# PSUM in two rings: side products share the four score banks, the scan's transposes keep the other three

## The chip, the cores and the metric

One core of a Trainium2 chip runs one fused kernel. The metric is the device time in microseconds of that core. PE is TensorE (its weight loads are listed apart as PEld), DVE is VectorE, ACT is ScalarE, POOL is GpSimd and SP is the engine that issues most DMAs. Each engine has one queue and works it off in order.

## The reference

The input x is 4 images of 64 x 64 positions and 256 channels, in float32. Two layers follow each other.

```python
# layer 0: a gated block with a scan over 2x2 windows and a depthwise convolution
x_norm = layernorm(x); x_proj, z = split(x_norm @ in_proj_W)          # 256 -> 384 + 384
y_ssm = 0.5 * (scan_fwd(windows(x_proj)) + scan_bwd(windows(x_proj))) # 4 steps, 8 states per channel
y_conv = gelu(depthwise3x3(x_proj) @ pw_W)
y = (alpha * y_ssm + (1 - alpha) * y_conv) * silu(z) @ out_W
x = x + y
x = x + gelu(layernorm(x) @ fuse_W1 + b1) @ fuse_W2 + b2
# layer 1: attention over all 4096 positions of an image
f, g, h = x @ Wf + bf, x @ Wg + bg, x @ Wh + bh                       # 32, 32, 256 channels
out = gamma * (softmax(g @ f.T) @ h @ Wo + bo) + x
```

The scan's step is `state = exp(dt * a) * state + dt * b * x`, and its output is `sum(state * c)` over the 8 states.

## The kernel before, in words

Layer 0 works on 32 blocks of 512 positions (8 rows of an image), 8 blocks to an image. The work of a block is a Python generator that yields a cost in microseconds after each piece, and generators are interleaved by these costs, so that the program's order is a planned mixture; a scheduler of the building layer then fixes the order on each engine and adds the semaphores.

The scan of a block (`scan`, L394) is the backbone. For each of 24 steps and two directions, ACT computes decays (`decays`, L368), PE transposes them in three 128 x 128 pieces into a PSUM tile `pa` (`turned`, L434), DVE multiplies `pa` into the state (`decayed`, L442 and L446) and then updates output and state (L452, L461). Beside the scan, `side` (L688) runs the rest of the neighbouring blocks: layer norm and projections (`to_channels` L273, `head` L302, `gate` L317), the scan's inputs (`prepare` L334 to L354), the depthwise convolution on PE and DVE (L550, L567), `tail` with its matmuls (L598, L623, L643, L654, L667, L678). `inputs` (L389) and `merge` (L539) are transposes at the ends of a scan.

As soon as the first image is through layer 0, attention begins, and `attend` (L994) becomes the outer loop: for each block of 128 queries, 8 times four matmuls of exponentials with values into `acc` (L1008), then a piece of `weights` for the next queries, then 7.2 us worth of layer 0 (`fill(RATE)`). `weights` (L804) makes the next queries' exponentials in 8 such pieces: twice 16 small score matmuls (L816, 32 rows each, four side by side, each of the four into a bank of its own), the maximum over the keys by DVE (L824) and a copy to SBUF by ACT (L827); then the maximum over partitions by a transpose, a reduction and a broadcast (L836 to L844), and then four times an addition by DVE and an exponential by ACT (L847, L848). The exponential tiles `eq` have seven buffers. When layer 0 is through, `attend_late` (L972) and `late_weights` (L893) do the rest with 256 queries at a time.

PSUM has eight banks, which are handed out so:

- pool `ps`, a ring of three banks (`bank`, L144): every product of the side work, `inputs`, `merge`, and the scan's `pa` in all blocks but the first eight;
- pool `pss`, two pairs of two banks (`pair`, L156): the scores, and the two small tiles of the maximum. In the first eight blocks, before there are any scores, the scan's `pa` lie here, the two directions of a step in one pair (`place`, L420);
- pool `pso`, one bank: `acc`.

A tile's bank is free once the engine that reads it (DVE or ACT) is through, and PE, which works in order, waits at the first matmul into a bank that isn't free.

Of the kernel before, what the change touches and what calls it, by code (L numbers as in the profile page):

```python
# [23 lines left out]
ALU = mybir.AluOpType  # L24
# [35 lines left out]
def block_then_attention_kernel(  # L60
# [94 lines left out]

    def pair(i):  # L156
        return pss.tile([P, 2, TOK], F32, tag=f"pair{i}", name=f"pair{i}")

# [109 lines left out]
    def to_channels(dst, src):  # L268

        for k in range(KD):  # L270
            pt = bank()
            for t in range(4):
                nc.tensor.transpose(pt[:, t * P : (t + 1) * P], src[:, t, k * P : (k + 1) * P], ident)  # L273
            nc.scalar.copy(dst[:, k, :], pt)
            yield 0.44
# [15 lines left out]
    def head(at):  # L291

        xt = heads.pop(at)
        layernorm(xt, xt)
        yield 5.0
        xnT = two.tile([P, KD, TOK], F32, tag="xnT", name="xnT")
        yield from to_channels(xnT, xt)
        xc = three.tile([P, KI, TOK], F32, tag="xc", name="xc")
        for f in range(KI):
            pp = bank()  # L300
            for k in range(KD):
                nc.tensor.matmul(  # L302
                    pp, lhsT=win[:, k, f * P : (f + 1) * P], rhs=xnT[:, k, :],
                    start=(k == 0), stop=(k == KD - 1),
                )
            nc.scalar.activation(xc[:, f, :], pp, AF.Identity, bias=b_in[:, f : f + 1])
            yield 1.72
        heads[at] = xnT, xc
        ready["head"] = at

    def gate(at, whole):
        xnT = heads[at][0]
        zs = one.tile([P, KI, TOK], F32, tag="zs", name="zs")
        for f in range(KI):
            pz = bank()
            for k in range(KD):
                nc.tensor.matmul(  # L317
                    pz, lhsT=win[:, k, INNER + f * P : INNER + (f + 1) * P], rhs=xnT[:, k, :],
                    start=(k == 0), stop=(k == KD - 1),
                )  # L320
            nc.scalar.activation(zs[:, f, :], pz, AF.Silu, bias=b_in[:, KI + f : KI + f + 1])
            if not whole:
                yield 1.72
        gates[at] = zs
        if whole:
            yield 5.2

    def prepare(at):

        _, xc = heads[at]  # L330

        pj = bank()
        for k in range(KI):
# [3 lines left out]
        yield 2.58  # L337
        pbc = ps.tile([P, 4, 2, 64], F32, tag="ps", name="pbc")
        for t in range(4):
# [10 lines left out]
        for d in range(2):  # L350
            dts.append(two.tile([P, KI, TOK], F32, tag="dt", name="dt"))
            for f in range(KI):
                pd = bank()
                nc.tensor.matmul(  # L354
                    pd, lhsT=wdt[64 * d : 64 * d + RANK, f * P : (f + 1) * P],
                    rhs=proj[64 * d : 64 * d + RANK, :], start=True, stop=True,
                )
                nc.scalar.activation(dts[d][:, f, :], pd, AF.Silu, bias=v("dt_b_b" if d else "dt_b_f", f))
            if at >= NBLK:
                yield 1.7  # L360
# [33 lines left out]
    def scan(at, ensue):  # L394
# [22 lines left out]

        pairs = {}

        def place(d, j):  # L420

            if at >= NBLK:
                return bank()
            if j + d not in pairs:
                pairs[j + d] = pair((j + d) % 2)
            return pairs[j + d][:, d, :]

# [115 lines left out]
    def depthwise(ydw, dense):  # L543

        for f in range(KI):
            if f < dense:
                pc = bank()
                for tap in range(9):
                    dy, dx = divmod(tap, 3)
                    nc.tensor.matmul(  # L550
                        pc, lhsT=diags[9 * f + tap], rhs=xp[:, f, dy : dy + ROWS, dx : dx + W],
                        start=(tap == 0), stop=(tap == 8),
                    )
                    if tap in (2, 5):
                        yield 2.6
                nc.scalar.copy(ydw[:, f, :], pc)
                yield 2.6
                continue
# [28 lines left out]
    def tail(at):  # L587
# [7 lines left out]
        for f in range(KI):  # L595
            pw = bank()
            for k in range(KI):
# [20 lines left out]
        for t2 in range(2):  # L618
            po = ps.tile([P, 2, DIM], F32, tag="ps", name="po")
            for t1 in range(2):  # L620
                t = 2 * t2 + t1
                for k in range(KI):
                    nc.tensor.matmul(  # L623
                        po[:, t1, :], lhsT=yz[:, k, t * P : (t + 1) * P], rhs=wout[:, k, :],
                        start=(k == 0), stop=(k == KI - 1),
                    )
            nc.vector.tensor_tensor(xo[:, 2 * t2 : 2 * t2 + 2, :], po, xo[:, 2 * t2 : 2 * t2 + 2, :], ALU.add)
            yield 3.2
# [11 lines left out]
        for f in range(KF):  # L640
            pf = bank()
            for k in range(KD):
# [6 lines left out]
        for t2 in range(2):  # L649
            pq = ps.tile([P, 2, DIM], F32, tag="ps", name="pq")  # L650
            for t1 in range(2):
# [12 lines left out]
        yield from to_channels(xT, xo)  # L664
        pf = bank()
        for k in range(KD):
# [8 lines left out]
        for t in range(4):  # L675
            po = bank()
            for k in range(KD):
# [126 lines left out]
    def weights(b, q, es):  # L804
# [3 lines left out]
        for g in range(2):  # L808
            pr = [pair(i) for i in range(2)]

            with tc.high_priority():
                last = None
                for s in range(4):
                    at = g * TOK + s * P
                    for r in (2, 3, 0, 1):
                        ins = nc.tensor.matmul(  # L816
                            pr[r // 2][:, r % 2, s * P : (s + 1) * P], lhsT=fQ[CK * r : CK * (r + 1), at : at + P],
                            rhs=gq[CK * r : CK * (r + 1), :], start=True, stop=True,
                        )
                        last = behind(ins, last)  # L820
            mx = two.tile([P, 2, P], F32, tag="mx", name="mx")
            for a in range(2):
                e = ep.tile([P, 2, TOK], F32, tag="eq", name="eq")
                nc.vector.tensor_reduce(  # L824
                    mx[:, a, :], pr[a].rearrange("p r (s q) -> p q (r s)", s=4), AX.X, ALU.max
                )
                nc.scalar.copy(e, pr[a])  # L827
                es.append(e)
            if g == 0:
                mx0 = mx  # L830
            yield
            yield
        nc.vector.tensor_tensor(mx0, mx0, mx, ALU.max)
        pm = pair(0)
        for c in range(2):
            nc.tensor.transpose(pm[:, 0, c * P : (c + 1) * P], mx0[:, c, :], ident)  # L836
        nm = st.tile([P, 1], F32, tag="nm", name="nm")
        nc.vector.tensor_reduce(nm, pm[:, 0, :QB], AX.X, ALU.max, negate=True)
        nmb = two.tile([P, P], F32, tag="nb", name="nmb")
        nc.vector.tensor_copy(nmb, nm.to_broadcast([P, P]))  # L840
        pn = pair(1)
        nc.tensor.matmul(pn[:, 0, :P], lhsT=nmb, rhs=ident, start=True, stop=True)
        nb = two.tile([P, P], F32, tag="nb", name="nb")
        nc.scalar.copy(nb, pn[:, 0, :P])  # L844
        for n, e in enumerate(es):
# [47 lines left out]
    def late_weights(b, q, odd, es):  # L893
# [6 lines left out]
        for g in range(4):  # L900
            pr = [pair(i) for i in range(2)]
            for s in range(2):
                at = (g // 2) * TOK + (2 * (g % 2) + s) * P
                for r in range(4):
                    nc.tensor.matmul(  # L905
                        pr[r // 2][:, r % 2, s * QB : (s + 1) * QB], lhsT=fQ[CK * r : CK * (r + 1), at : at + P],
                        rhs=gq[CK * r : CK * (r + 1), :], start=True, stop=True,
                    )
            for a in range(2):
                pool, tag = SLOTS[8 * odd + 2 * g + a]  # L910
                e = pool.tile([P, 2, 2, QB], F32, tag=tag, name="eT")
                for j in range(2):
                    nc.scalar.copy(e[:, j], pr[a][:, j, :].rearrange("p (s q) -> p s q", s=2))  # L913
                if g == 0 and a == 0:
# [9 lines left out]
        nc.vector.tensor_tensor(m2, mx[:, 0, :], mx[:, 1, :], ALU.max)  # L924
        pm = pair(0)
        for c in range(2):
            nc.tensor.transpose(pm[:, 0, c * P : (c + 1) * P], m2[:, c * P : (c + 1) * P], ident)
        nm = st.tile([P, 2], F32, tag="nm", name="nm")
        nc.vector.tensor_reduce(
            nm, pm[:, 0, :QB].rearrange("p (c k) -> p c k", c=2), AX.X, ALU.max, negate=True  # L930
        )
# [3 lines left out]
        yield  # L935
        pn = pair(1)
        for c in range(2):
            nc.tensor.matmul(
                pn[:, 0, c * P : (c + 1) * P], lhsT=wide[:, c, :], rhs=ident, start=True, stop=True
            )  # L940
        nb = two.tile([P, QB], F32, tag="mx", name="nb")
        nc.scalar.copy(nb, pn[:, 0, :QB])  # L942
        for n, e in enumerate(es):
# [214 lines left out]
```

## Time and profile before

| | |
|---|---|
| time, median of 3 runs | 5544.09 us (5538.5 to 5545.41) |
| the profiled execution | 5536.67 us, of it 5534.9 us span |
| PE busy | 5111.2 us (92%) |
| DVE busy | 4585.6 us (83%) |
| ACT busy | 3626.7 us (66%) |

The profile shows one execution. It is read in three stages: up to about 1000 us layer 0 runs alone (the first image), from there to about 4566 us layer 0 of the other images runs beside attention, and from 4566 us on attention runs alone. A row of the groups of instructions gives the line, the engine, what it writes and reads, the count, the busy time, the mean duration of one, and the idle time of its engine just before with what ended it. PE runs a float32 matmul as two instructions of the trace, a transpose as one. A row of the waits names who waited for whom, the sum in microseconds, how often, and the longest.

### The profile page before, as it was taken

How to read it: one execution, taken by the hardware profiler on the slowest of the kernel's cores; microseconds unless marked ns; L12 is line 12 of the kernel's file. 1: busy time of each engine (PE TensorE's matmuls, PEld its weight loads, DVE VectorE, ACT ScalarE, POOL GpSimd, SP SyncE). 2: the span in 40 equal slices, each digit the busy share in tenths (PEclk: the TensorE clock that was granted, in tenths of full speed). 3: DMA queues.
4: the chain of work that ended last, by engine and by line, in shares of the span. 5: the costliest groups of instructions: out<-in, count | busy, mean ns of one | idle time of the engine just before them, and what ended most of it. 6: DMA issues, size and time to landing. Idle time of an engine off the chain costs nothing. (4 is left out here: it accounts for less than half of the span.)

```text
span 5534.9 us, 77215 instructions
## 1 busy us (share of the span) xinstructions
PE 5111.2 (92%) x27476; PEld 3619.7 (65%) x27476; DVE 4585.6 (83%) x8158; ACT 3626.7 (66%) x5248; POOL 202.6 (4%) x304
## 2 busy tenths in 40 slices
PE   7888888899999999999999999999999999999999
PEld 4555555566666666666666666666666667888887
DVE  6888888889888898988988888899988885666665
ACT  5666667666666777777667776777677654555444
POOL 0000000000000000000000000000000000000000
PEclk7999999899999999999999999999999999999999
DMA  1000100133333333433333333333333335555554
GB/s 46 25 22 24 32 18 18 50 109 112 102 111 114 108 107 115 118 110 114 113 109 108 117 113 115 109 106 117 115 115 106 105 106 160 148 144 146 147 146 138
DMA packets 333121, 558.42 MB, mean 101 GB/s; under 512 B 51904, under 2 KB 86976, under 8 KB 332736
## 3 DMA queue, kind: packets, MB, share of 16 engines
q1 hardware_dynamic: 330160, 551.52, 33.7%
q8 instruction: 218, 3.57, 0.3%
q10 hardware_dynamic: 2576, 1.97, 0.1%
q14 instruction: 167, 1.37, 0.1%
HBM read 494.49 MB, written 58.79 MB: 100 GB/s over the span
## 5 line engine op out<-in xcount | busy, mean ns | idle before, releaser
L1008 PE MATMUL acc<-vt,eq 128*128 128x257 f32 x4864 | 1231.9, 388 | 24.8 <-issue 14.0
L373 ACT ACTIVATE e<-dt,a_sc 128x384 f32<-128x384 f32 x1536 | 855.1, 608 | 356.5 <-PE bank L434 270.8
L1008 PEld LDWEIGHTS acc<-vt,eq 128*128 128x128 f32 x4864 | 893.9, 194 | 234.5 <-issue 115.4
L452 DVE SCALAR_TENSOR_TENSOR y<-p,bc,y 128x384 f32<-128x384 f32 x1536 | 941.2, 613 | 1.2
L986 PE MATMUL bank<-vt,eT 128*128 128x257 f32 x2496 | 624.7, 382 | 0.0
L461 DVE SCALAR_TENSOR_TENSOR h<-u,bc,p 128x384 f32<-128x384 f32 x1024 | 620.5, 623 | 0.2
L434 PEld LDWEIGHTS bank<-ident,e 128*128 128x128 f32 x3456 | 412.1, 142 | 256.7 <-DVE p L442 74.0
L434 PE MATMUL bank<-ident,e 128*128 128x128 f32 x3456 | 511.6, 278 | 70.8 <-DVE p L442 46.6
L986 PEld LDWEIGHTS bank<-vt,eT 128*128 128x128 f32 x2496 | 467.0, 189 | 80.7 <-issue 12.9
L446 DVE TENSOR_TENSOR p<-bank,h 128x384 f32<-128x384 f32 x768 | 408.7, 548 | 104.0 <-PE bank L434 101.4
L827 ACT COPY eq<-pair 128x1024 f32<-128x1024 f32 x304 | 302.9, 1010 | 221.8 <-DVE mx L824 108.3
L373 ACT ACT_TABLE_LOAD x310 | 397.7, 1283 | 7.8 <-PE bank L434 2.6
L848 ACT ACTIVATE eq<-eq 128x1024 f32<-128x1024 f32 x304 | 317.5, 1055 | 116.3 <-DVE eq L847 108.6
L824 DVE TENSOR_REDUCE mx<-pair 128x128 f32<-128x1024 f32 x304 | 362.0, 1213 | 24.1 <-PE pair L816 24.0
L847 DVE TENSOR_TENSOR eq<-eq,nb 128x1024 f32<-128x1024 f32 x304 | 361.8, 1227 | 18.7 <-ACT nb L844 17.8
L918 DVE TENSOR_TENSOR mx<-mx,eT 128x512 f32<-128x512 f32 x364 | 251.9, 692 | 140.4 <-ACT eT L913 110.6
L913 ACT COPY eT<-pair 128x512 f32<-128x512 f32 x416 | 213.1, 598 | 184.3 <-PE pair L905 184.3
L567 DVE SCALAR_TENSOR_TENSOR ydw<-xp,vec,ydw 128x512 f32<-128x512 f32 x448 | 320.8, 744 | 2.9
L598 PE MATMUL bank<-ydw,wpw 128*128 128x512 f32 x576 | 274.4, 608 | 21.6 <-DVE p L446 17.5
L442 DVE SCALAR_TENSOR_TENSOR p<-bank,bc,u 128x384 f32<-128x384 f32 x384 | 233.7, 608 | 67.2 <-PE bank L434 67.0
L945 DVE TENSOR_TENSOR eT<-eT,nb 128x1024 f32<-128x1024 f32 x208 | 238.5, 1218 | 46.9 <-ACT nb L942 46.9
L550 PE MATMUL bank<-xp,dw 128*128 128x512 f32 x576 | 274.6, 603 | 1.7 <-DVE xc L540 1.7
(150 smaller groups left out, 7775.5 us busy)
## 6 DMA issues: line engine op xcount, KB each, us to landing
vt<-vod SPq DMA_DIRECT2D x1632, 257.0 KB, 2.8
vod<-vst SPq DMA_DIRECT2D x32, 514.0 KB, 4.3
xo<-in_x_dram SPq DMA_DIRECT2D x256, 64.0 KB, 2.6
xt<-in_x_dram SPq DMA_DIRECT2D x256, 64.0 KB, 1.9
x1d<-xo SPq DMA_DIRECT2D x32, 512.0 KB, 2.9
res<-x1d SPq DMA_DIRECT2D x76, 128.0 KB, 2.7
out_dram<-res SPq DMA_DIRECT2D x304, 32.0 KB, 1.6
fgd<-fg SPq DMA_DIRECT2D x32, 256.0 KB, 2.1
```

What stands on the lines that cost most here:

```text
L373: nc.scalar.activation(e[:, f, :], dts[d][:, f, lo : lo + 3 * P], AF.Exp, scale=a_sc[:, d, f * NST + n : f * NST + n + 1],)
L434: nc.tensor.transpose(pa[:, f * P : (f + 1) * P], es[d, n][:, f, off : off + P], ident)
L446: nc.vector.tensor_tensor(p, pa[:, :INNER], hs[d], ALU.mult)
L452: nc.vector.scalar_tensor_tensor(y[:, t, :], p, bc[:, t, d, NST + n : NST + n + 1], y[:, t, :], ALU.mult, ALU.add)
L461: nc.vector.scalar_tensor_tensor(hs[d], u[d][:, t, :], bc[:, t, d, n : n + 1], p, ALU.mult, ALU.add)
L567: nc.vector.scalar_tensor_tensor(o, x_tap, w_tap, o, ALU.mult, ALU.add)
L824: nc.vector.tensor_reduce(mx[:, a, :], pr[a].rearrange("p r (s q) -> p q (r s)", s=4), AX.X, ALU.max)
L827: nc.scalar.copy(e, pr[a])
L847: nc.vector.tensor_tensor(e8, e8, nb.unsqueeze(1).broadcast_to([P, 8, P]), ALU.add)
L848: nc.scalar.activation(e, e, AF.Exp)
L986: nc.tensor.matmul(sums[c][:, : DIM + 1], lhsT=e[:, r % 2, s, c * P : (c + 1) * P], rhs=vt[:, s, :], start=(n == 0 and s == 0), stop=(n == ...
L1008: nc.tensor.matmul(acc[:, : DIM + 1], lhsT=es[k // 2][:, k % 2, a : a + P], rhs=vt[:, s, :], start=(n == 0 and s == 0), stop=(n == 2 * NI ...
```

## The change

The two pairs become four single banks with the tags q0 to q3. `aside()` hands them out in turn. All side products (L273, L302, L317, L334, L340, L354, L550, L598, L623, L643, L654, L667, L678) and the two small tiles of the maximum now take the next of these four. The ring of three is left to the scan's `pa`, `inputs` and `merge`; in the first eight blocks every fourth `pa` goes to the bank of `acc`, which is not yet in use. The scores take all four banks at once (`four`), the bank that was handed out last coming first, and do not move the turn.

In `weights`, ACT copies each score bank by itself (four copies of 512 columns instead of two of 1024), and DVE takes the maximum a piece later, from the copies in SBUF instead of from PSUM. The number of pieces stays 8; the steps L833 to L844 come one piece earlier. `late_weights` takes the four single banks too; its copies were of single banks already.

```diff
-    def pair(i):
-        return pss.tile([P, 2, TOK], F32, tag=f"pair{i}", name=f"pair{i}")
+    turn = [0]
+    def aside(shape=(P, TOK)):
+        i = turn[0]
+        turn[0] = (i + 1) % 4
+        return pss.tile(list(shape), F32, tag=f"q{i}", name=f"q{i}")
+    def four():
+        return [
+            pss.tile([P, TOK], F32, tag=f"q{i}", name=f"q{i}") for i in ((turn[0] - 1 - r) % 4 for r in range(4))
+        ]
...
-            pt = bank()
+            pt = aside()
...
         def place(d, j):
-            if at >= NBLK:
-                return bank()
-            if j + d not in pairs:
-                pairs[j + d] = pair((j + d) % 2)
-            return pairs[j + d][:, d, :]
+            if at < NBLK and (2 * j + d) % 4 == 3:
+                return pso.tile([P, TOK], F32, tag="pso", name="pa")
+            return bank()
...
         for g in range(2):
-            pr = [pair(i) for i in range(2)]
+            pr = four()
...
-                    for r in (2, 3, 0, 1):
+                    for r in range(4):
...
-                            pr[r // 2][:, r % 2, s * P : (s + 1) * P], lhsT=fQ[CK * r : CK * (r + 1), at : at + P],
+                            pr[r][:, s * P : (s + 1) * P], lhsT=fQ[CK * r : CK * (r + 1), at : at + P],
...
             for a in range(2):
                 e = ep.tile([P, 2, TOK], F32, tag="eq", name="eq")
+                for j in range(2):
+                    nc.scalar.copy(e[:, j, :], pr[2 * a + j])
+                es.append(e)
+            yield
+            for a in range(2):
                 nc.vector.tensor_reduce(
-                    mx[:, a, :], pr[a].rearrange("p r (s q) -> p q (r s)", s=4), AX.X, ALU.max
+                    mx[:, a, :], es[2 * g + a].rearrange("p r (s q) -> p q (r s)", s=4), AX.X, ALU.max
                 )
-                nc.scalar.copy(e, pr[a])
-                es.append(e)
             if g == 0:
                 mx0 = mx
-            yield
-            yield
+                yield
...
-        nc.scalar.copy(nb, pn[:, 0, :P])
+        nc.scalar.copy(nb, pn[:, :P])
+        yield
```

The other edits replace `bank()`, `ps.tile(...)` or `pair(i)` by `aside()` in the places listed above, in the same manner as the first of them.

More of the change, by code (lines that the diff above doesn't have):

```diff
@@ L299, in head @@
         for f in range(KI):
-            pp = bank()
+            pp = aside()
             for k in range(KD):
@@ L314, in gate @@
         for f in range(KI):
-            pz = bank()
+            pz = aside()
             for k in range(KD):
@@ L330, in prepare @@
         _, xc = heads[at]
-        pj = bank()
+        pj = aside()
         for k in range(KI):
@@ L337, in prepare @@
         yield 2.58
-        pbc = ps.tile([P, 4, 2, 64], F32, tag="ps", name="pbc")
+        pbc = aside((P, 4, 2, 64))
         for t in range(4):
@@ L352, in prepare @@
             for f in range(KI):
-                pd = bank()
+                pd = aside()
                 nc.tensor.matmul(
@@ L416, in scan @@
         hs = {}
-        pairs = {}
         def place(d, j):
-            if at >= NBLK:
-                return bank()
-            if j + d not in pairs:
-                pairs[j + d] = pair((j + d) % 2)
-            return pairs[j + d][:, d, :]
+            if at < NBLK and (2 * j + d) % 4 == 3:
+                return pso.tile([P, TOK], F32, tag="pso", name="pa")
+            return bank()
         def turned(d, j):
@@ L546, in depthwise @@
             if f < dense:
-                pc = bank()
+                pc = aside()
                 for tap in range(9):
@@ L595, in tail @@
         for f in range(KI):
-            pw = bank()
+            pw = aside()
             for k in range(KI):
@@ L618, in tail @@
         for t2 in range(2):
-            po = ps.tile([P, 2, DIM], F32, tag="ps", name="po")
+            po = aside((P, 2, DIM))
             for t1 in range(2):
@@ L640, in tail @@
         for f in range(KF):
-            pf = bank()
+            pf = aside()
             for k in range(KD):
@@ L649, in tail @@
         for t2 in range(2):
-            pq = ps.tile([P, 2, DIM], F32, tag="ps", name="pq")
+            pq = aside((P, 2, DIM))
             for t1 in range(2):
@@ L664, in tail @@
         yield from to_channels(xT, xo)
-        pf = bank()
+        pf = aside()
         for k in range(KD):
@@ L675, in tail @@
         for t in range(4):
-            po = bank()
+            po = aside()
             for k in range(KD):
@@ L823, in weights @@
                 e = ep.tile([P, 2, TOK], F32, tag="eq", name="eq")
+                for j in range(2):
[3 more added lines that the diff above has]
+            for a in range(2):
                 nc.vector.tensor_reduce(
-                    mx[:, a, :], pr[a].rearrange("p r (s q) -> p q (r s)", s=4), AX.X, ALU.max
+                    mx[:, a, :], es[2 * g + a].rearrange("p r (s q) -> p q (r s)", s=4), AX.X, ALU.max
                 )
-                nc.scalar.copy(e, pr[a])
-                es.append(e)
             if g == 0:
                 mx0 = mx
-            yield
-            yield
+                yield
         nc.vector.tensor_tensor(mx0, mx0, mx, ALU.max)
-        pm = pair(0)
+        pm = aside()
         for c in range(2):
-            nc.tensor.transpose(pm[:, 0, c * P : (c + 1) * P], mx0[:, c, :], ident)
+            nc.tensor.transpose(pm[:, c * P : (c + 1) * P], mx0[:, c, :], ident)
         nm = st.tile([P, 1], F32, tag="nm", name="nm")
-        nc.vector.tensor_reduce(nm, pm[:, 0, :QB], AX.X, ALU.max, negate=True)
+        nc.vector.tensor_reduce(nm, pm[:, :QB], AX.X, ALU.max, negate=True)
         nmb = two.tile([P, P], F32, tag="nb", name="nmb")
         nc.vector.tensor_copy(nmb, nm.to_broadcast([P, P]))
-        pn = pair(1)
-        nc.tensor.matmul(pn[:, 0, :P], lhsT=nmb, rhs=ident, start=True, stop=True)
+        pn = aside()
+        nc.tensor.matmul(pn[:, :P], lhsT=nmb, rhs=ident, start=True, stop=True)
         nb = two.tile([P, P], F32, tag="nb", name="nb")
-        nc.scalar.copy(nb, pn[:, 0, :P])
+        nc.scalar.copy(nb, pn[:, :P])
+        yield
         for n, e in enumerate(es):
@@ L900, in late_weights @@
         for g in range(4):
-            pr = [pair(i) for i in range(2)]
+            pr = four()
             for s in range(2):
@@ L905, in late_weights @@
                     nc.tensor.matmul(
-                        pr[r // 2][:, r % 2, s * QB : (s + 1) * QB], lhsT=fQ[CK * r : CK * (r + 1), at : at + P],
+                        pr[r][:, s * QB : (s + 1) * QB], lhsT=fQ[CK * r : CK * (r + 1), at : at + P],
                         rhs=gq[CK * r : CK * (r + 1), :], start=True, stop=True,
@@ L912, in late_weights @@
                 for j in range(2):
-                    nc.scalar.copy(e[:, j], pr[a][:, j, :].rearrange("p (s q) -> p s q", s=2))
+                    nc.scalar.copy(e[:, j], pr[2 * a + j].rearrange("p (s q) -> p s q", s=2))
                 if g == 0 and a == 0:
@@ L924, in late_weights @@
         nc.vector.tensor_tensor(m2, mx[:, 0, :], mx[:, 1, :], ALU.max)
-        pm = pair(0)
+        pm = aside()
         for c in range(2):
-            nc.tensor.transpose(pm[:, 0, c * P : (c + 1) * P], m2[:, c * P : (c + 1) * P], ident)
+            nc.tensor.transpose(pm[:, c * P : (c + 1) * P], m2[:, c * P : (c + 1) * P], ident)
         nm = st.tile([P, 2], F32, tag="nm", name="nm")
         nc.vector.tensor_reduce(
-            nm, pm[:, 0, :QB].rearrange("p (c k) -> p c k", c=2), AX.X, ALU.max, negate=True
+            nm, pm[:, :QB].rearrange("p (c k) -> p c k", c=2), AX.X, ALU.max, negate=True
         )
@@ L935, in late_weights @@
         yield
-        pn = pair(1)
+        pn = aside()
         for c in range(2):
             nc.tensor.matmul(
-                pn[:, 0, c * P : (c + 1) * P], lhsT=wide[:, c, :], rhs=ident, start=True, stop=True
+                pn[:, c * P : (c + 1) * P], lhsT=wide[:, c, :], rhs=ident, start=True, stop=True
             )
         nb = two.tile([P, QB], F32, tag="mx", name="nb")
-        nc.scalar.copy(nb, pn[:, 0, :QB])
+        nc.scalar.copy(nb, pn[:, :QB])
         for n, e in enumerate(es):
```

## The prediction, as it was put on record

> **What bounds the kernel now.** I read the busy times by stage first, then PE's waits in the two early stages, then DVE's and ACT's waits, then a stretch of the timeline. The busy times (stretch, length, PE, PEld, DVE, ACT, POOL busy, each with its count, then PE's clock and the DMAs):
>
> ```profile
> 0.00:1000.00 1000.00, 849.51 (x3373) 518.37 (x3374) 834.22 (x1688) 658.70 (x1036) 55.54 (x87) 0.91 0.08 26
> 1000.00:4566.00 3566.00, 3308.81 (x18557) 2325.91 (x18555) 3155.34 (x5615) 2502.44 (x3534) 142.75 (x211) 0.98 0.37 109
> 4566.00:5535.00 969.00, 952.93 (x5550) 775.44 (x5548) 596.03 (x856) 465.53 (x680) 4.29 (x7) 0.99 0.51 147
> ```
>
> PE is the fullest engine: it idles 150, 257 and 16 us in the three stages. Stage 3 offers nothing. DVE idles 166 and 411 us in the first two, so it comes close behind. All that can be won at an unchanged amount of PE work is some 400 us. PE's longest waits, stage 1 (first two lines) and stage 2:
>
> ```profile
> PE pair L434 <- DVE p L446: 38.1, 29, 2.7
> PE bank L354 <- ACT dt L358: 19.7, 16, 2.0
> ...
> PE bank L434 <- DVE p L442: 46.2, 38, 3.0
> PE bank L598 <- DVE p L446: 17.5, 15, 2.2
> ...
> PE bank L273 <- DVE p L446: 13.2, 12, 1.9
> PE pair L816 <- ACT eq L827: 10.4, 11, 1.9
> PE bank L317 <- ACT u L390: 8.9, 9, 1.9
> ```
>
> None of these is a wait for data: a pointwise matmul (L598) doesn't read what L446 writes. L446 had to read a transpose before its bank could be used again. Adding the rows of stage 2 whose releaser isn't an input of the waiting matmul gives about 180 of 257 us. The timeline shows how it comes about:
>
> ```profile
> 2202.66 4.63 DVE L847 TENSOR_TENSOR eq<-eq,nb 128x1024 f32<-128x1024 f32 x4 [0.88 <-ACT nb L844]
> ...
> 2207.21 2.35 DVE L824 TENSOR_REDUCE mx<-pair 128x128 f32<-128x1024 f32 x2
> ...
> 2209.48 0.60 DVE L442 SCALAR_TENSOR_TENSOR p<-bank,bc,u 128x384 f32<-128x384 f32 x1
> ...
> 2210.14 1.98 PE L643 MATMUL bank<-h2T,wf 128*128 128x512 f32 x4 [1.54 <-DVE p L442]
> ```
>
> For 7 us DVE is on attention's additions and maxima, two transposes stay unread in the ring of three, and a side product stands for 1.54 us before a bank.
>
> [...] adding 512 columns takes 687 ns from PSUM (L658) and 683 ns from SBUF (L386).
>
> **The change part by part.** The instrument is a count. Along PE's order in both built programs I added up PE work between the last matmul into a bank and the first of the next tile there. Back to back, the timeline gives 0.14 us per transpose (6 in 0.82), 0.47 per `acc` matmul (8 halves in 1.90), about 0.45 for 256 columns, 0.89 for 512 and 0.07 for a score matmul. I then took the mean wait in front of such tiles in the trace of before, by that distance (under 1, 1–2, 2–3, 3–6, over 6 us) and by who empties the bank.
>
> *Stage 2, ordinary reuse.* Before, ACT-emptied: 10/92/246/362/228 tiles with mean waits 0.24/0.24/0.07/0.04/0.03 us; DVE-emptied: 81/228/360/666/123 with 0.19/0.27/0.17/0.05/0.01. Together 237 us, nearly all of PE's idle time. After: 1/30/55/148/276 and 4/43/98/460/814. The same means give 26 + 60 = 86 us, so **−151**. Bounds: nothing of it, if the waits move to DVE (a rival below), and −180, all bank waits.
>
> *Stage 1* in the same way: before 10/77/59/115/60 tiles at 0.24/0.31/0.25/0.02/0.02 and 38/57/28/126/105 at 1.1/0.28/0.32/0.10/0, 125 us; after 9/19/33/123/130 and 8/57/44/186/240, 77 us: **−48**. Bounds 0 and −85 (its bank waits).
>
> *What the scores now wait for.* They need all four q banks. In 55 of 152 groups less than 1 us of PE work lies between a side product's last matmul and the score matmul on its bank. Emptying takes 0.69 us (L647) plus ACT's lag. The trace of before shows that lag (end of the matmul to start of the evacuation) as 0.3 us on average for L274, 0.7 for L306, 1.0 for L390, and 1.6 for L647 and L358, which have a table load ahead; without these about 0.5. At 1.2 us in all the missing time adds up to 22 us; before it was 11: **+11** (0 to +48).
>
> *What waits for the scores.* Before, pairs were reused 20 us later; ACT could copy when it liked (in the middle 10 us later). Now side products queue for these banks. In 95 of 152 groups the first needs the bank that is copied last, and in 108 it comes less than 2 us of PE work after the scores, typically two `acc` matmuls and six transposes (0.95 + 0.82 = 1.77 us). Four copies at 598 ns (L913, the same 512-column copy) take 2.39 us. With a lag of 0.5, typically 2.9 − 1.8 = 1.1 us is missing. Summed group by group: 73 us at no lag, 101 at 0.3, 124 at 0.5, 185 at 1.0, 288 at 1.8. I take 0.5: **+124**. Behind the waiting product PE's whole queue stands, `acc` and transposes too; DVE goes on with the two or three transposes that it has.
>
> *ACT.* 304 x (2 x 598 − 1010) = 57 us more, on an engine busy 70% of stage 2; outside the hand-over hidden. Its waits for L824 (104 us) go. So do those for an `eq` buffer that `acc` frees (94 us): in PE's new order the buffer's last reader comes after the scores in 8 of 297 cases, before in 159.
>
> *DVE.* The maximum from SBUF: 0 by the 4 ns above[...]; I take 0. Because the maximum comes a piece later, runs of three or more of L824/L847 between two reads of transposes fall from 65 to 34. My means contain the old runs: **−15** (0 to −40).
>
> *Stage 3.* PE is busy 953 of 969 us and the copies are as before: 0 (−5 to +10). DMA issues, matmuls and transposes are the same in number.
>
> Sum: −151 − 48 + 11 + 124 − 15 = −79, so 5537 − 79 = 5458 for an execution like the profiled one. That one lies 7 us under the median; against the median I forecast **5465 us**, 1.4% less, with 5425 to 5510 for this case.
>
> **The rivals.** *The scores' hand-over eats it all (slower).* If ACT comes to the copies as late as it does to L647, L358 or L603 now (1.6 to 1.9 us), the hand-over costs 288: 5544 − 151 − 48 + 11 + 288 − 15 = 5629, say **5630**. It decides from a mean lag of about 1.15 us, where it costs 203. For it: table loads of 1.28 us stand in ACT's queue. Against: copies need none, and ACT loses 198 us of waits ahead of them.
>
> *The hand-over is cheap.* With ACT at once ready, 73 instead of 124, and no wait ahead of the scores (−11 instead of +11): 5544 − 151 − 48 − 11 + 73 − 15 = 5392, **5392**. For it: ACT waits for PE in most places now.
>
> *DVE becomes the bound.* It is busy 88% of stage 2; PE may run ahead and then wait for L442/L446 all the same. Then only part of DVE's wait for transposes in stage 2 (161 us) goes. With a fifth, −30: **5514**.
>
> *That the change doesn't do what it says* is excluded by the built order: all side products stand on q tiles, and the short distances have gone.
>
> **How the numbers follow.** Likeliest case 0.48, cheap hand-over 0.20, DVE the bound 0.12 (nearly half of that within 0.2%), slower 0.20. A measurement of this kernel can tell about 0.2% (11 us) from no change. Faster is 0.48 + 0.20 + 0.05 = 0.73 and same 0.07. The range 5390 to 5600 leaves out about a tenth below (half the cheap case) and a tenth above (half the slower one).
>
> **What would show it.** PE's waits on DVE L442/L446 in front of side products (L598, L273, L302, L643) should be near nothing, and those of L434 under 20 us. New rows of side products waiting for the score copy should hold 70 to 180 us, each 0.5 to 1.5 us. PE's idle time in stage 1 should fall to about 100 us; ACT's waits for the maximum and for `acc` should be gone. I am wrong if the score copy's rows exceed 200 us, or if PE's waits for L442/L446 stay.

## The result and the profile after

The changed kernel takes 5543.99 us (median of 12 runs, 5538.61 to 5548.57); the kernel before, run beside it, 5543.56 us (12 runs, 5534.12 to 5546.32). The ratio is 1.0002, 95% interval 0.9993 to 1.0011: no change, where 5465 us was forecast.

That is not because nothing happened. In both kernels the matmul for the eighth block's queries and keys (L667 before, L674 after) marks the end of the first image, and that of the 32nd block the end of layer 0. The first mark moved from 1014 to 920 us, the second from 4595 to 4601. Stage 1 won 94 us, and stage 2 lost 100. (The profiled executions took 5536.67 us before and 5548.57 after, 7 under and 5 over their medians, so some 12 us of the difference between the two traces is spread of executions. By the medians stage 2 lost about 88.) The busy times between these marks, first of the kernel before, then of the kernel after (stretch, length, PE, PEld, DVE, ACT, POOL, then PE's clock and the DMAs):

```profile
0.00:1014.00 1014.00, 862.89 (x3436) 528.18 (x3437) 844.69 (x1710) 667.07 (x1051) 56.83 (x89) 0.91 0.08 26
1014.00:4595.00 3581.00, 3321.34 (x18614) 2334.00 (x18613) 3156.10 (x5616) 2503.08 (x3530) 145.76 (x215) 0.98 0.37 109
```

```profile
0.00:920.00 920.00, 832.97 (x3402) 515.60 (x3403) 835.89 (x1696) 641.51 (x1034) 55.83 (x87) 0.93 0.09 28
920.00:4601.00 3681.00, 3359.27 (x18587) 2378.89 (x18586) 3347.30 (x5625) 2469.46 (x3797) 147.69 (x217) 0.96 0.36 107
```

Between the marks of stage 2 DVE has nearly the same number of instructions as before (5625 against 5616) and is busy 191 us longer. One row of the groups explains it. The maximum over the scores, before (from the pair in PSUM) and after (from the copy in SBUF):

```profile
L824 DVE TENSOR_REDUCE mx<-pair 128x128 f32<-128x1024 f32 x304 | 362.0, 1213 | 24.1 <-PE pair L816 24.0
```

```profile
L836 DVE TENSOR_REDUCE mx<-eq 128x128 f32<-128x1024 f32 x304 | 572.5, 1917 | 82.2 <-ACT eq L832 81.8
```

The same reduction of the same 1024 columns takes 1.92 us instead of 1.21, every one of them (1.86 to 1.98), and so 210 us more in all.

On PE the 100 us of stage 2 appear in two parts: it idles 322 us instead of 260, and its busy time grows from 3321 to 3359 us for nearly the same number of records, while its granted clock falls from 0.98 to 0.96. Rows of waits show the first part only.

PE's waits in stage 2 of the kernel after, the longest rows (waits are summed over 1000 to 4566 us, as in the prediction):

```profile
PE q L845 <- DVE mx L842: 82.7, 38, 4.7
PE q L851 <- DVE nmb L849: 26.2, 25, 3.0
PE bank L441 <- DVE p L449: 22.9, 9, 3.5
PE bank L441 <- DVE p L453: 19.7, 14, 3.1
PE q L605 <- ACT eq L832: 17.6, 17, 2.4
PE q L630 <- ACT eq L832: 15.2, 12, 2.6
PE bank L400 <- DVE uT L397: 12.0, 4, 5.3
PE q L661 <- ACT eq L832: 10.1, 12, 2.0
```

No side product waits for a scan transpose to be read any more; the rows of before are gone. In their place stand the wait for the score copies (L832; all such rows of side products together 71 us) and, at the top, one that the prediction doesn't have: PE's transposes of the maximum (L845) wait for L842, the maximum over DVE's two partial results. The timeline of the kernel after shows one:

```profile
3324.90 3.67 DVE L836 TENSOR_REDUCE mx<-eq 128x128 f32<-128x1024 f32 x2
...
3328.48 0.56 DVE L453 TENSOR_TENSOR p<-bank,h 128x384 f32<-128x384 f32 x1
3328.94 0.42 DVE L842 TENSOR_TENSOR mx<-mx 128x256 f32<-128x256 f32 x1
...
3329.42 0.69 PE L845 MATMUL q<-ident,mx 128*128 128x128 f32 x2 [4.71 <-DVE mx L842]
```

Two reductions of 1.9 us stand ahead of L842, and PE's whole queue waits 4.71 us for it. ACT's waits for the maximum and for `acc` are gone, as forecast (198 us before, 2.5 us left).

### The profile page after: what moved, and what is told of

Read it like the earlier page. It is cut to its first block, busy times and chain, and to the rows that moved or that the text cites. A ratio compares the mean times of both kernels' runs of the same rounds, so it can differ in the third digit from the quotient of the medians.

```text
span 5546.8 us, 77289 instructions
## 1 busy us (share of the span) xinstructions
PE 5125.2 (92%) x27476; PEld 3653.9 (66%) x27476; DVE 4778.7 (86%) x8158; ACT 3570.1 (64%) x5508; POOL 203.5 (4%) x304
## 5 line engine op out<-in xcount | busy, mean ns | idle before, releaser
L1018 PEld LDWEIGHTS acc<-vt,eq 128*128 128x128 f32 x4864 | 913.6, 197 | 236.0 <-issue 102.3
L441 PEld LDWEIGHTS bank<-ident,e 128*128 128x128 f32 x4320 | 531.1, 145 | 339.9 <-issue 141.7
L441 PE MATMUL bank<-ident,e 128*128 128x128 f32 x4320 | 662.5, 283 | 88.2 <-DVE p L453 39.9
L836 DVE TENSOR_REDUCE mx<-eq 128x128 f32<-128x1024 f32 x304 | 572.5, 1917 | 82.2 <-ACT eq L832 81.8
L453 DVE TENSOR_TENSOR p<-bank,h 128x384 f32<-128x384 f32 x960 | 516.9, 554 | 41.6 <-PE bank L441 39.2
L832 ACT COPY eq<-q 128x512 f32<-128x512 f32 x608 | 311.2, 593 | 173.8 <-PE q L823 163.8
L923 ACT COPY eT<-q 128x512 f32<-128x512 f32 x416 | 213.1, 597 | 188.6 <-PE q L915 188.6
L449 DVE SCALAR_TENSOR_TENSOR p<-bank,bc,u 128x384 f32<-128x384 f32 x480 | 294.8, 614 | 35.4 <-PE bank L441 33.6
L605 PE MATMUL q<-ydw,wpw 128*128 128x512 f32 x576 | 276.7, 610 | 22.1 <-ACT eq L832 18.1
L557 PE MATMUL q<-xp,dw 128*128 128x512 f32 x576 | 273.0, 595 | 1.6 <-ACT eq L832 1.6
```

The source lines that it names most:

```text
L441: nc.tensor.transpose(pa[:, f * P : (f + 1) * P], es[d, n][:, f, off : off + P], ident)
L453: nc.vector.tensor_tensor(p, pa[:, :INNER], hs[d], ALU.mult)
L832: nc.scalar.copy(e[:, j, :], pr[2 * a + j])
L836: nc.vector.tensor_reduce(mx[:, a, :], es[2 * g + a].rearrange("p r (s q) -> p q (r s)", s=4), AX.X, ALU.max)
L1018: nc.tensor.matmul(acc[:, : DIM + 1], lhsT=es[k // 2][:, k % 2, a : a + P], rhs=vt[:, s, :], start=(n == 0 and s == 0), stop=(n == 2 * NI ...
```

## The experiments

Theory 1: the two rings do what was forecast, and the maximum, strided in SBUF, gave the gain back. Theory 2: the hand-over of the score banks between scores and side products gave it back. Theory 3: DVE bounds stage 2 whatever the maximum costs. Lines of the experiments' kernels differ by a few from those of the kernel after. Where a ratio is given, it is to the kernel before, run beside it on the same chip (5538.44 us beside the first four, 5537.3 beside the others).

**Another maximum, all else as changed.** DVE takes element-wise maxima of whole score copies, whose columns lie side by side. Two small tiles of `late_weights` get another buffer with it; stage 3 stays at 946 us.

```diff
-            for a in range(2):
-                nc.vector.tensor_reduce(
-                    mx[:, a, :], es[2 * g + a].rearrange("p r (s q) -> p q (r s)", s=4), AX.X, ALU.max
-                )
+            if g == 0:
+                nc.vector.tensor_tensor(mx, es[0][:, 0, :], es[0][:, 1, :], ALU.max)
+            for h in range(2 if g == 0 else 0, 4):
+                nc.vector.tensor_tensor(mx, mx, es[2 * g + h // 2][:, h % 2, :], ALU.max)
...
-        nc.vector.tensor_tensor(mx0, mx0, mx, ALU.max)
+        nc.vector.tensor_tensor(mx[:, :QB], mx[:, :QB], mx[:, QB:], ALU.max)
```

> The changed kernel with one edit: DVE takes the maximum over the score copies as seven element-wise maxima of 512 contiguous columns (about 0.69 us each by the row of L928) in place of four strided reductions (1.92 us each). DVE work per block of 128 queries falls from 4 x 1.92 + 0.45 = 8.1 us to 7 x 0.69 + 0.42 = 5.3 us, about 215 us in all; PSUM rings and score copies stay. Theory 1 (the strided maximum from SBUF ate the gain): stage 2 no longer loses 105 us against the kernel before, time 5400 to 5460 us. Theory 2 (the hand-over of the score banks ate it): the waits for the score copies stay and the time stays above 5515 us. Theory 3 (DVE bounds stage 2 whatever the maximum costs): 5500 to 5530 us.

Measured: 5398.21 us, ratio 0.9742 (0.9728 to 0.9757), just below the expected range. The new maxima take 0.69 us each (shortest, median and longest in ns):

```profile
L837 DVE TENSOR_TENSOR mx<-eq x76: 655/692/700, 930.8 to 4460.6; 128x512 f32<-128x512 f32 x76
L839 DVE TENSOR_TENSOR mx<-mx,eq x456: 668/688/1226, 931.9 to 4471.4; 128x512 f32<-128x512 f32 x152
```

Busy times between the same two marks:

```profile
0.00:919.00 919.00, 831.68 (x3404) 514.87 (x3404) 835.96 (x1697) 641.68 (x1035) 55.76 (x87) 0.93 0.09 29
919.00:4437.00 3518.00, 3284.70 (x18583) 2336.28 (x18584) 3133.87 (x5846) 2475.89 (x3804) 152.86 (x217) 0.98 0.38 111
```

DVE is back at 3134 us, and stage 2 lasts 3518 us: 163 less than in the kernel after, 63 less than before. This profiled execution (5384.37 us) lies 14 us under its median; by the medians the experiment wins 146 us on the kernel after, and stage 2 is about 50 us shorter than before. Of the 163 us, 88 are PE's idle time (322 to 233 us) and 75 its busy time (3359 to 3285 us), which falls by 2.2% while the clock rises by about 2%, from 0.96 to 0.98. The clock goes with the kernel: its mean over the whole execution was 0.962 to 0.965 in all 12 runs of the kernel after and 0.972 to 0.975 in all four here. So the strided maximum cost PE idle time and speed as well; why less clock was granted with it, the runs don't show.

The hand-over is unchanged: its rows (L605, L630, L661 and others) still add up to 71 us. So theory 2 is out as the cause, and theory 3 too. PE's longest waits in stage 2:

```profile
PE q L845 <- DVE mx L842: 37.5, 29, 3.2
PE q L605 <- ACT eq L833: 20.1, 17, 2.4
PE bank L441 <- DVE p L453: 13.8, 8, 3.1
PE q L851 <- DVE nmb L849: 13.8, 13, 3.2
PE q L630 <- ACT eq L833: 12.8, 11, 2.6
PE bank L441 <- DVE p L449: 11.5, 7, 2.4
```

**The strided maximum alone, in the kernel before.**

```diff
-                nc.vector.tensor_reduce(
-                    mx[:, a, :], pr[a].rearrange("p r (s q) -> p q (r s)", s=4), AX.X, ALU.max
-                )
                 nc.scalar.copy(e, pr[a])
+                nc.vector.tensor_reduce(
+                    mx[:, a, :], e.rearrange("p r (s q) -> p q (r s)", s=4), AX.X, ALU.max
+                )
```

> The kernel before with one edit: ACT copies the pair first and DVE reduces the copy in SBUF instead of the pair in PSUM; rings and pieces as before. Theory 1: each of the 304 reductions takes 1.92 instead of 1.21 us, DVE gets 214 us more to do in stage 2 where it idled 411 us, and the kernel is slower by 60 to 150 us (5605 to 5695 us). Theory 2: the place of the maximum matters little, within 20 us of the kernel before.

Measured: 5678.81 us, ratio 1.0250 (1.0233 to 1.0267), 140 us more, with PSUM shared out as before. (The order of copy and maximum is exchanged with it, so the 140 us are the sum of both.) Stage 1 is as before (1013 us), stage 2 takes 3719 us, 138 more:

```profile
1013.00:4732.00 3719.00, 3369.57 (x18615) 2359.22 (x18616) 3359.34 (x5615) 2508.59 (x3536) 143.51 (x215) 0.96 0.36 105
```

DVE's 203 us of additional work cost 138 us, although DVE had idled 425 us of this stage: two thirds of an addition to the second-fullest engine came through. On PE 90 of them are idle time and 48 a longer busy time, again with a clock of 0.96 instead of 0.98.

**The disputed cost by itself.** A kernel with DVE reductions alone.

```python
    def view(t, s):
        return t.rearrange("p (h x s) -> p h s x", x=8, s=s)   # the 8 elements of a maximum lie s floats apart
...
            nc.vector.tensor_reduce(o.rearrange("p (h s) -> p h s", s=s), view(src, s), AX.X, ALU.max)
```

> DVE alone, nothing of the reference but the shapes: maxima over 8 of 1024 columns with the elements of one maximum 1, 2, 4, 8, 16, 32, 64 or 128 floats apart, from SBUF, and 1, 2, 8 and 128 from PSUM; element-wise maximum and copies with a stride of 128 floats. If the access pattern in SBUF is what costs (theory 1a): 1.92 us at a distance of 128 and about 1.21 at a distance of 1 from SBUF, 1.21 at any distance from PSUM. If it is contention with the other engines in the full kernel (theory 1b): 1.21 us everywhere here. If it is that a reduction from SBUF is slow whatever the distance (theory 1c): 1.92 us for all from SBUF.

Measured, by groups (rsb: from SBUF, rpu: from PSUM; the last letter is the distance, b = 1, c = 2, d = 4, e = 8, i = 128 floats; ttcont and ttstrided are element-wise maxima, all contiguous and with one operand at a distance of 128):

```profile
L81 DVE TENSOR_REDUCE rsbe<-sb 128x128 f32<-128x1024 f32 x6 | 11.9, 1977 | 0.0
L81 DVE TENSOR_REDUCE rsbd<-sb 128x128 f32<-128x1024 f32 x6 | 11.8, 1959 | 0.0
...
L92 DVE TENSOR_TENSOR ttstrided<-sb,sb 128x1024 f32<-128x1024 f32 x6 | 11.5, 1919 | 0.0
...
L81 DVE TENSOR_REDUCE rsbi<-sb 128x128 f32<-128x1024 f32 x6 | 11.2, 1867 | 0.0
...
L81 DVE TENSOR_REDUCE rpui<-pu 128x128 f32<-128x1024 f32 x6 | 7.5, 1256 | 0.1
...
L81 DVE TENSOR_REDUCE rpub<-pu 128x128 f32<-128x1024 f32 x6 | 7.3, 1222 | 0.0
L89 DVE TENSOR_TENSOR ttcont<-sb,sb 128x1024 f32<-128x1024 f32 x6 | 7.3, 1221 | 0.0
L81 DVE TENSOR_REDUCE rsbc<-sb 128x128 f32<-128x1024 f32 x6 | 7.3, 1214 | 0.0
L81 DVE TENSOR_REDUCE rsbb<-sb 128x128 f32<-128x1024 f32 x6 | 7.3, 1214 | 0.0
```

With PE idle throughout and ACT idle from 17 us on, the reduction takes 1.87 us at the kernel's distance of 128 floats, and 1.21 at 1 or 2. Where two of them stand close in time, the distance still decides: the last reduction at a distance of 2 started at 18.1 us and took 1.21 us, the first at 4 started at 19.3 and took 1.96; the last `ttcont` started at 98.0 us (1.22) and the first `ttstrided` at 100.3 (1.92). So it is the access pattern (1a), not contention (1b), and not reductions from SBUF as such (1c). The step lies between 2 floats (1.21) and 4 (1.96); why there, is not shown. From PSUM the distance costs nearly nothing (1.22 to 1.27 us at 1, 2, 8 and 128).

**One ring in stage 2.** On top of the first experiment: once the scores have begun, side products go back to the ring of three.

```diff
     def aside(shape=(P, TOK)):
+        if began[0]:
+            return ps.tile(list(shape), F32, tag="ps", name="bank")
```

> e1_tree, but from the first scores on all side products go back to the ring of three that the scan's transposes use, and the four q banks are left to the scores alone: two rings in stage 1, one ring in stage 2, no hand-over. Theory 1: stage 1 keeps its 94 us, stage 2 is as in the kernel before, so about 5450 us, slower than e1_tree by what the two rings are worth in stage 2 (I expect 20 to 50 us). Theory 2: without the hand-over it is faster than e1_tree by 50 to 80 us. Theory 3: the same as e1_tree within 15 us.

Measured: 5486.62 us, ratio 0.9907 (0.9892 to 0.9921). Stage 1 keeps its gain (921 us); stage 2 takes 3620 us, 102 more than with two rings (88 by the medians) and 39 more than before. Theory 2 had forecast a gain, but this is no clean price of the second ring: one row dominates PE's waits, that of scores for the copies of earlier scores.

```profile
PE q L829 <- ACT eq L839: 90.0, 60, 3.9
PE bank L447 <- DVE p L455: 25.0, 19, 3.3
```

Besides this wait (90 us instead of 10) the score matmuls are busy 274 us instead of 190. Together that is more than the whole loss, and PE's idle time as a whole is even lower than in the first experiment (216 against 233 us). So the scores of this kernel, which stand close behind the copies, cost more than the 102 us, and the run doesn't price the second ring. Why they stand so is not shown.

**The hand-over.** On top of the first experiment: the bank that the next side product takes, the last in the list, is copied first and not last.

```diff
-                for j in range(2):
-                    nc.scalar.copy(e[:, j, :], pr[2 * a + j])
                 es.append(e)
+            for h in (3, 2, 1, 0):
+                nc.scalar.copy(es[2 * g + h // 2][:, h % 2, :], pr[h])
```

> e1_tree with the four score copies in the other order, so that the bank which the next side product takes is copied first. Tells what the hand-over of the score banks to the side products costs. Theory 1 (the hand-over costs PE the 70 us or so that it shows as waiting for the score copies, and nothing else makes up for it): these waits fall to under 25 us and the kernel gains 30 to 60 us on e1_tree (5340 to 5370 us). Theory 3 (DVE or the chain of the maximum bounds stage 2 now, so that PE's waits are only shifted): the waits fall, the time stays within 15 us of e1_tree.

Measured: 5362.86 us, ratio 0.9685 (0.9671 to 0.9700), 35 us less than the first experiment. The side products' waits for the copies fall from 71 to 46 us, not under 25: the longest row is now that of L328, 14.7 us, which had been 7.9. I take it that side products which came second before now come before their bank's copy; this is not shown. The time falls by about as much as these waits (35 us by the medians, 22 between the two profiled executions), so the waits are real costs, and theory 3 is wrong here too.

**The maximum from the score banks, ahead of the copies.** The first experiment's maxima read the banks in PSUM; those over the copies in SBUF go.

```diff
+                nc.vector.tensor_copy(mx, pr[0])
...
                 for j in range(2):
+                    if g or a or j:
+                        nc.vector.tensor_tensor(mx, mx, pr[2 * a + j], ALU.max)
                     nc.scalar.copy(e[:, j, :], pr[2 * a + j])
```

> e1_tree with the maxima taken from the score banks themselves, ahead of each bank's copy: one copy and seven maxima of 512 columns from PSUM, at about 0.69 us each as from SBUF, so DVE has only 0.3 us more per block of queries (19 us in all). Tells why the maximum could not simply stay in PSUM beside the two rings. Theory 1: the side products now wait until DVE, which came to the scores 5.7 us late on average in the kernel before, and then ACT are through with the banks; PE's waits behind the scores grow, slower than e1_tree by 50 to 200 us. Theory 2b (where the maximum is read does not matter as long as it isn't strided in SBUF): within 25 us of e1_tree.

Measured: 5489.51 us, ratio 0.9912 (0.9897 to 0.9926), 91 us more than the first experiment. The side products' waits for the score copies grow from 71 to 124 us. The copies themselves wait for DVE (engine idle ahead of L836, the copy):

```profile
  DVE mx L835: 277.4, 230
  DVE mx L830: 128.6, 51
```

PE idles 48 us more than in the first experiment in stage 2, and is busy 64 us longer at a clock of 0.97 instead of 0.98. So taking the maximum out of PSUM was right for the hand-over, as far as this order of maxima and copies tells, and only the way it reads SBUF was wrong.

**What stage 1 gained from.** Stage 1 with single banks for the transposes but the ring of three for everything else; stage 2 as in the first experiment.

```diff
     def aside(shape=(P, TOK)):
+        if not began[0]:
+            return ps.tile(list(shape), F32, tag="ps", name="bank")
...
-            if at < NBLK and (2 * j + d) % 4 == 3:
-                return pso.tile([P, TOK], F32, tag="pso", name="pa")
+            if at < NBLK:
+                i = (2 * j + d) % 4
+                return pss.tile([P, TOK], F32, tag=f"q{i}", name="pa")
```

> e1_tree with another stage 1: there the scan's transposes take four single score banks in turn, and side products share the ring of three with the stage's other transposes, as in the kernel before but with single banks in place of the pairs. Stage 2 as in e1_tree. Tells what the 94 us of stage 1 come from. Theory S1 (the pairs, free only when both directions are read, held PE up: its waits at the pair for L446 and L442 are 44 us): most of the 94 us stays, within 25 us of e1_tree. Theory S2 (the side products' own four banks bring it): stage 1 falls back towards the kernel before, 60 to 94 us slower than e1_tree.

Measured: 5479.11 us, ratio 0.9896 (0.9882 to 0.9910), 81 us more than the first experiment. Stage 1 takes 1012 us, 2 less than before. Theory S1 falls: parting the pairs by itself brings next to nothing (PE idles 131 us instead of 151, but is busy 18 us longer, with its clock at 0.89 instead of 0.91). The 94 us come from the way the banks are shared out: the side products have four to themselves and no longer stand in one ring with `inputs` and `merge`, and the bank of `acc` is used too. Which of these brings how much was not tried.

**The maximum's chain one piece later.** On top of the reversed copies.

```diff
-            if g == 0:
-                yield
+            yield
...
-            yield
+            if n != 1:
+                yield
```

> e5_tree_rev with the transpose, reduction and broadcast of the maximum one piece later, apart from DVE's maxima (the second and third addition then share a piece). PE's transposes stood there behind DVE's maxima for 37 us (L845) and 14 us (L851) in e1_tree. Theory 1: these waits fall to under 15 us, 20 to 50 us faster than e5_tree_rev. Theory 3: within 15 us of it.

Measured: 5340.43 us, ratio 0.9646 (0.9633 to 0.9659), 22 us less. PE's waits at the transposes and the broadcast (here L844 and L850) are 9 and 17 us: the first fell from 31, the second rose from 7. This is the fastest version found, 3.5% under the kernel before.

## Why the prediction was wrong, step by step

| step | forecast | what the runs show |
|---|---|---|
| stage 1, ordinary reuse | −48 | −94 (1014 to 920 us): PE's idle time −64, its busy time −30 |
| stage 2, waits for DVE to read transposes | most of −151 | rows for L442/L446 from 107 to about 45 us, 26 without the strided maximum |
| in front of the scores | +11 | +4 (rows of L816 10.7, of L823 14.6) |
| hand-over of the score banks | +124 | rows of 71 us |
| DVE: the maximum from SBUF | 0 | +191 us of DVE work, +146 us of time by the medians |
| DVE: shorter runs of additions and maxima | −15 | not measured by itself |
| the maximum's chain a piece earlier | not costed | L845/L851 wait 111 us, before 5; 51 without the strided maximum |
| stage 2 together | −31 | without the strided maximum −63 in the traces, about −50 by the medians; with it +100, about +88 by the medians |

**The step that failed** is the one under "DVE" in the prediction: "The maximum from SBUF: 0 by the 4 ns above", and then "I take 0". The 4 ns compare an addition (L658) with what is in truth a multiplication (L386), and the operands of both lie contiguously. The reduction reads 128 floats apart, and for that the trace of before has no row from SBUF; the one row that looked like it, L824, read PSUM. The prediction had the price of contiguous reads alone, so a price above 0 was never in the sum. Two experiments price the step from both sides: taking it out of the changed kernel wins 146 us (5544.0 to 5398.2), putting it alone into the kernel before costs 140 us. A second term was left out: the maximum's chain comes a piece earlier, close behind DVE's maxima. Moving it back wins 22 us (5362.86 to 5340.43), with contiguous maxima.

The signs named in the prediction could not show this. The waits for the score copies stayed far under 200 us, side products no longer waited for transposes to be read, and PE's idle time in stage 1 fell to 87 us, as forecast; only the waits of L434 (L441 after) stayed at 43 us instead of under 20. All of these watch waits, and none watches DVE's busy time.

**The mechanism of the rings was right and its size too small.** Without the strided maximum the change brings 2.6%, not 1.4%. In stage 1 the gain of 94 us lies outside the forecast's bounds (0 to −85). The forecast priced PE's idle time alone; yet PE's busy time fell by 30 us as well. PE's clock was granted at 0.93 instead of 0.91, which by estimate (833 us times 0.02/0.91, if busy time goes with the clock) is worth some 18 of the 30, and 34 records fewer lie ahead of the mark (3402 against 3436, at 0.25 us each another 8). DVE too has 1% fewer instructions there (1696 against 1710), so up to about 10 of the 94 us may be work that has moved behind the mark. In stage 2 the hand-over was overpriced by about 50 us, while the waits for transposes to be read fell by 81 us of their 107 once the strided maximum was gone.

**The rivals.** "DVE becomes the bound" (5514 us) came nearest, for a reason that it didn't name: DVE had more to do. The slower rival, the hand-over, had the right place, but its rows came to 71 us in the kernel after, not to 288. That the measured time lies between these two rivals is luck: the term that decided stands in neither.

## What to carry to other kernels

A step moved to another memory is a new operation: price it with its access pattern, from a row that has that pattern, and bound it from above where there is none. When a large change moves the time by nothing, set marks in both traces at the same piece of work and take the difference at each: a gain in one stage and a loss in the next show at once. An engine's idle time was no reserve here: of 203 us added to DVE, which idled 425, 138 arrived in the time. And look at the busiest engine's busy time and clock beside its waits: here nearly half of what the strided maximum cost in stage 2 (75 of 163 us) stood in no row of waits.

## What the runs showed of the hardware

A DVE reduction of 1024 floats from SBUF took 1.85 to 1.98 us with the elements of a maximum 4, 8, 16, 32, 64 or 128 floats apart, and 1.21 us at 1 or 2; an element-wise maximum took 1.92 us with one operand at a distance of 128 and 1.22 with both contiguous. From PSUM the reduction took 1.22 to 1.27 us at every distance tried (1, 2, 8 and 128). Contiguous reductions from the two memories differed by 8 ns (1214 and 1222). DVE's copy with a distance of 128 floats took 1.30 us, against 1.23 for its contiguous copy from SBUF to PSUM, so the loss was not the same in every operation. ACT's copy with that distance took 1.95 us; a contiguous one from SBUF was not measured.

In the traces of before and after each engine started its work in the order of the built program: all 27476 matmul records of PE, all 8158 instructions of DVE, ACT's 4567 (before) and 4871 (after) beside its table loads, POOL's 297 and 298 of the kernel's own lines, and SP's 3195 DMA issues.
